# Three-layer feature-cross kernel: fc's columns loaded word by word, dummy products moved and added, and a new order of POOL's first transfers

## The chip, the cores and the metric

The kernel runs on one core of a Trainium2 chip. The metric is the device time of one execution in microseconds; the time before is the median of 8 runs. Five engines work side by side, each on its own list of instructions: TensorE (PE, with its weight loads as PEld), VectorE (DVE), ScalarE (ACT), GpSimd (POOL) and SyncE (SP). SP, ACT and POOL also issue the transfers (DMAs). One execution was also taken by the profiler; all single durations below come from it.

## The reference

The input x has 1024 samples of F = 39 fields with E = 64 values. Three layers each multiply every field of the layer before with every field of x, value by value, and mix the products with a weight table of 64 rows. The sums over E of all three layers' rows go through one linear output, fc.

```python
def _cin_layer(Xk, X0, W, b):
    O = W.shape[0]
    Hk, Fdim = (Xk.shape[1], X0.shape[1])
    Wr = W.reshape(O, Hk, Fdim)
    return jnp.einsum('bhe,bfe,ohf->boe', Xk, X0, Wr) + b[None, :, None]

X0 = sparse_embedding
Xk = X0
outs = []
for W, b in ((W0, b0), (W1, b1), (W2, b2)):
    Xk = _cin_layer(Xk, X0, W, b)
    outs.append(Xk.sum(axis=-1))
cin_output = jnp.concatenate(outs, axis=-1)
return cin_output @ fc_w.T + fc_b
```

fc_w has 192 values: 64 for each layer. Called fc's columns below, they are 64 words each, one for each row of a layer.

## The kernel before

Since the output is linear in the last layer, the kernel folds the weights before it touches the data. fc's third column times W2 gives V2 (one value per row of layer 2 and field; line 338, into the PSUM banks `pv`). V2, with fc's second column beside it as a fortieth column, times W1 gives a second table (line 389, banks `pt` and `pv`). Transposed, it stands in `both` beside the transposed W0 (line 349). From `both`, sums along diagonals (`weight_rows`, lines 436 and 440) and seven 128x128 turns (`weight_turn`, lines 471 and 472) make the stationary operands `wa` of the main part. This is the prologue, some 20 us.

The main part goes through 32 blocks of 32 samples (2048 columns each). A product of two fields is symmetric, so each block needs each pair of fields once; the pairs fill six chunks of 128 rows and half of a seventh, which two blocks share. For each chunk DVE multiplies two gathered copies of the block's rows (`product`, line 164, or 166 for the shared chunk), and TensorE multiplies the result with `wa` (line 487): four 512-column matmuls of two passes each. ACT and DVE finish a block (`finish`, lines 506 to 517): the upper 64 rows plus fc0s, times the lower 64 plus b0s, summed over E. Three small matmuls at the end (line 624) add up the rows of `sums` with `wfin`, which line 532's `last_weights` makes from V2, the biases and `fc`.

The gathered copies are made by POOL with indirect transfers (`gather_rows`, line 125) from tables in device memory that hold a block's 39 rows and a fortieth row of ones. The index lists are worked out by DVE at the start. Block 0 comes in two halves through the tables `xh`, so that the first six gathers (lines 322 to 324) can start before the block is in `xd`; SP copies `xh` into `xd` (line 328). ACT's queue loads W2, xh's first half, W0, W1 and xh's second half, in this order.

The order on each engine is written out by hand: an engine runs its instructions in the order of the program text, and waits where data are missing. On TensorE the prologue is: dummies (`spin`, line 230, products of constants whose result nobody reads), the small products, one dummy, V2 (line 338), W0's transposes (349), W1's product (389), the turns of its result (409), dummies, the first weight turn (471), a dummy, and the main products.

The small products turn fc's row on one partition into columns. SP loads fc_w into `fcrow` (line 193). POOL doubles the third column into `fcrow2` (284) and makes a mask of even and odd rows (281, 282). TensorE turns `fcrow2` (298); DVE writes it, masked, into two columns of `fc2` (301), the stationary operand of V2's product: W2's 64 rows stand there as two halves each, on neighbouring partitions, so column 0 of `fc2` holds fc's column on the even rows and column 32 the same on the odd ones. Five more small products (296) turn the single columns into the PSUM bank `small`, from which ACT copies them into `v2` (362), `fc` (570) and `fc0s` (571).

Of the kernel before, what the change touches and what calls it, by code (L numbers as in the profile page):

```python
# [54 lines left out]
F32 = mybir.dt.float32  # L55
I32 = mybir.dt.int32
# [18 lines left out]
MM = 512  # L75
# [23 lines left out]
def cin_kernel(ctx: ExitStack, tc: tile.TileContext, x, w0t, b0, w1, b1, w2, b2, fc_w, fc_b, out):  # L99
# [39 lines left out]
    fc = const.tile([H, 3], F32, name="fc")  # L139
# [30 lines left out]
    with prep as prep:  # L170
# [4 lines left out]
        fcrow = prep.tile([1, 3 * H], F32, name="fcrow")  # L175
        fcrow2 = prep.tile([1, H, 2], F32, name="fcrow2")
# [6 lines left out]
        parity = prep.tile([128, 2], I32, name="parity")  # L183
        mask = prep.tile([128, 2], F32, name="mask")
# [3 lines left out]
        nc.vector.memset(ones, 1.0)  # L188
        nc.vector.memset(fc2, 0.0)
        nc.vector.memset(v2, 0.0)  # L190
        nc.vector.memset(warm, 0.0)
        w0v = w0t.rearrange("b a h -> b (a h)")
        nc.sync.dma_start(fcrow, fc_w)
# [18 lines left out]
        for i in range(3):  # L212
            for k, by in enumerate((STEP[i + 1], BASE[i + 1], EXTRA[i + 1] - K)):
                nc.gpsimd.memset(shifts[:, k, i : i + 1], float(by))
        for k in range(2):
            nc.gpsimd.dma_start(xh[k][F:FT].rearrange("r (p c) -> p r c", c=128), ones[0:8, 0:1])
# [8 lines left out]
        small = bank("small")  # L225
# [12 lines left out]
        spin(3)  # L238
# [26 lines left out]
        nc.vector.tensor_scalar(parity[:, 1:2], place, 1, None, ALU.bitwise_and)  # L265
# [15 lines left out]
        nc.gpsimd.tensor_copy(mask[:, 1:2], parity[:, 1:2])  # L281
        nc.gpsimd.tensor_scalar(mask[:, 0:1], mask[:, 1:2], -1.0, 1.0, ALU.mult, ALU.add)
        for s in range(2):
            nc.gpsimd.tensor_copy(fcrow2[:, :, s], fcrow[:, 2 * H : 3 * H])

# [3 lines left out]
        for k in range(NTAB):  # L289
            nc.gpsimd.dma_start(xd[k][F::FT].rearrange("r (p c) -> p r c", c=128), ones)  # L290


        one = ones[0:1, 0, 0:1]

        def turn_row(dst, k):
            nc.tensor.matmul(dst, fcrow[:, k * H : k * H + H], one, start=True, stop=True)  # L296

        nc.tensor.matmul(  # L298
            small[:, 0:1], fcrow2.rearrange("p h s -> p (h s)"), one, start=True, stop=True
        )  # L300
        nc.vector.tensor_scalar(fc2[:, 0::32], mask, small[:, 0:1], None, ALU.mult)  # L301
        nc.vector.tensor_scalar(unit, apart, 0, None, ALU.is_equal)
        for k in range(3):
            turn_row(small[0:H, k + 1 : k + 2], k)
        for k in range(2):
            turn_row(small[H:128, k + 4 : k + 5], k)
        spin()
# [14 lines left out]
        for k, cols in enumerate(halves):  # L322
            for i in range(3):
                gather_rows(rt[0][:, i, cols], xh[k], i)
            if not k:
                load(1, nc.gpsimd)
        for k, cols in enumerate(halves):
# [32 lines left out]
        for s, at in enumerate((2, 5)):  # L360
            rows = slice(H * s, H * s + H)
            nc.scalar.copy(v2[rows, s, F:FT], small[rows, at : at + 1])
# [6 lines left out]
        roll(1)  # L369
        for k, t in enumerate((b1, b2)):  # L370
            nc.gpsimd.dma_start(bias[:, k : k + 1], t.rearrange("(h o) -> h o", o=1))
        nc.gpsimd.dma_start(b0s, b0.rearrange("(h o) -> h o", o=1))
        nc.gpsimd.dma_start(fcb, fc_b.rearrange("(p o) -> p o", o=1))
# [14 lines left out]
        for k, a in groups:  # L388
# [6 lines left out]
            )  # L395

# [25 lines left out]
        spin()  # L422
        spin(1, MM // 4)
# [108 lines left out]
    def last_weights(pk):  # L532

        nc.tensor.matmul(pk[0:F, 0:1], v2[0:H, 0, 0:F], bias[:, 0:1], start=True, stop=True)
        nc.tensor.matmul(pk[0:1, 1:2], bias[:, 0:1], fc[:, 1:2], start=True, stop=False)
        nc.tensor.matmul(pk[0:1, 1:2], bias[:, 1:2], fc[:, 2:3], start=False, stop=True)
# [33 lines left out]
    nc.scalar.copy(fc, small[0:H, 1:4])  # L570
    nc.scalar.copy(fc0s[H:128], small[H:128, 4:5])
# [101 lines left out]
```

## Time and profile before

| | |
|---|---|
| median of 8 runs | 749.27 us (748.64 to 749.53) |
| profiled execution: its own time | 749.52 us |
| profiled execution: span | 747.7 us, so 1.8 us lie around it |
| TensorE (PE) busy | 742.8 us, 99% |
| DVE busy | 644.5 us, 86% |
| POOL busy | 321.9 us, 43% |
| ACT busy | 164.6 us, 22% |
| transfers | 180.40 MB, mean 241 GB/s |

How to read the profile's lines: a row of groups gives line, engine, operation, out<-in with partitions x elements and the count, then busy time in us, mean ns of one, then the idle time of that engine just before them and what ended it. The chain of work that ended last is followed back from the last instruction, at each step to what released it. A chain in order of time gives start, length and what ran. A busy PE is not PE at its peak: its clock can be granted at full or at half speed, which the windows view shows as a share in the column after POOL's.

### The profile page before, as it was taken

What the parts mean: (1) busy time and instruction counts of PE and PEld (TensorE: products, weight loads), DVE (VectorE), ACT (ScalarE), POOL (GpSimd) and SP (SyncE); (2) the same over time, 40 slices, a digit from 0 to 9 for tenths busy, and PEclk for the clock granted to TensorE, in tenths of its full rate; (3) what the DMA queues carried; (4) which work ended last, traced back from release to release, by engine and by line L of the source; (5) the groups of instructions that cost most, each with busy time, mean ns of one, the idle gap of its engine ahead of it and who ended that gap; (6) DMA issues with size and microseconds to landing.
All of it is one profiled execution on the core that took longest, in us unless ns stands there. A gap on an engine that the chain in (4) does not pass through costs nothing.

```text
span 747.7 us, 5258 instructions
## 1 busy us (share of the span) xinstructions
PE 742.8 (99%) x1895; PEld 327.4 (44%) x1895; DVE 644.5 (86%) x513; ACT 164.6 (22%) x226; POOL 321.9 (43%) x198
## 2 busy tenths in 40 slices
PE   8999999999999999999999999999999999999998
PEld 6444444444444444444444444444444444444443
DVE  6998889888889888898888889888899888899885
ACT  3132221221212222211221212222112221212222
POOL 7976633336344253633336243263533436243100
PEclk9999999999999999999999999999999999999999
DMA  9999775876657786575876657776565854737400
GB/s 297 345 296 412 258 281 176 330 259 227 277 163 273 250 312 240 182 280 179 338 253 222 270 167 280 259 277 246 190 285 193 337 224 185 283 136 297 168 1 0
DMA packets 58930, 180.40 MB, mean 241 GB/s; under 512 B 37172, under 2 KB 37237, under 8 KB 38808
## 3 DMA queue, kind: packets, MB, share of 16 engines
q0 software_dynamic: 24320, 169.44, 59.8%
q1 hardware_dynamic: 32894, 8.63, 5.0%
q10 hardware_dynamic: 1690, 1.99, 1.0%
q8 instruction: 15, 0.25, 0.1%
q14 instruction: 11, 0.09, 0.0%
HBM read 179.98 MB, written 10.60 MB: 255 GB/s over the span
## 4 chain that ended last, share of the span: by engine, by line
PE 99%; ACT 0%; DVE 0%; issue 0%; ACTq 0%
PE po L487 97%; PE idle L230 1%; PE pt L389 0%; PE pv L338 0%; PE pv L389 0%; PE pw L349 0%; ACT both L418 0%; PE tr L471 0%; ACT part L400 0%; PE small L296 0%; DVE g L526 0%; DVE sums L528 0%; ACT zq L525 0%; PE small L298 0%; DVE fc L301 0%
## 5 line engine op out<-in xcount | busy, mean ns | idle before, releaser
L487 PE MATMUL po<-p,wa 128*128 128x512 f32 (+1 forms) x1792 | 722.7, 595 | 0.0
L164 DVE TENSOR_TENSOR p<-r 128x2048 f32<-128x2048 f32 (+2 forms) x197 | 434.8, 2235 | 85.9 <-PE po L487 85.9
L487 PEld LDWEIGHTS po<-p,wa 128*128 128x128 f32 (+1 forms) x1792 | 313.9, 190 | 405.1 <-issue 384.0
L125 POOL DMA_INDIRECT r<-xd,lists x125 | 253.7, 2030 | 360.6 <-DVE p L164 334.4
L506 ACT ACTIVATE z<-po,fc0s 64x512 f32<-64x512 f32 x124 | 84.6, 683 | 356.5 <-PE po L487 349.7
L500 ACT COPY g<-u 39x1024 f32<-39x1024 f32 x64 | 66.7, 1043 | 180.2 <-DVE sums L517 178.6
L512 DVE SCALAR_TENSOR_TENSOR g<-po,b0s,z 64x512 f32<-64x512 f32 x124 | 86.4, 734 | 0.0
L517 DVE TENSOR_REDUCE sums<-g 103x16 f32<-103x1024 f32 x62 | 75.6, 1220 | 2.2
L166 DVE TENSOR_TENSOR p<-u,v 128x2048 f32<-128x2048 f32 x16 | 36.5, 2284 | 0.0
L125 POOL DMA_INDIRECT u<-xd,lists x16 | 28.9, 1803 | 4.9 <-issue 4.9
L125 POOL DMA_INDIRECT v<-xd,lists x16 | 20.8, 1302 | 4.9 <-issue 4.6
L526 DVE SCALAR_TENSOR_TENSOR g<-po,b0s,zq 64x512 f32<-64x512 f32 x4 | 3.0, 743 | 5.3 <-ACT zq L525 5.3
L230 PE MATMUL idle<-const-float32-1.0 128*128 128x256 f32 (+1 forms) x16 | 6.5, 555 | 0.8 <-PEq L660 0.8
L125 POOL DMA_INDIRECT r<-xh,lists x6 | 5.8, 971 | 1.9 <-issue 1.5
L472 ACT COPY wa<-tr 128x128 f32<-128x128 f32 x7 | 1.9, 266 | 19.4 <-PE tr L471 18.2
L436 DVE TENSOR_TENSOR pairs<-both 128x6 f32<-128x6 f32 (+27 forms) x50 | 5.4, 173 | 0.3 <-ACT both L418 0.3
L119 POOL DMA_DIRECT2D xd<-in_x x5 | 5.2, 1066 | 0.0
L525 ACT ACTIVATE zq<-po,fc0s 64x512 f32<-64x512 f32 x4 | 2.7, 683 | 10.2 <-PE po L487 10.2
L230 PEld LDWEIGHTS idle<-const-float32-1.0 128*128 128x128 f32 x16 | 4.3, 295 | 1.4 <-issue 0.7
L471 PE MATMUL tr<-unit,pairs 128*128 128x128 f32 x7 | 2.2, 319 | 0.9 <-ACT pairs L440 0.9
L528 DVE TENSOR_REDUCE sums<-g 103x8 f32<-103x512 f32 x4 | 2.7, 686 | 0.1
L624 PE MATMUL py<-sums,wfin 103*1 103x512 f32 (+2 forms) x6 | 2.1, 448 | 0.6 <-DVE sums L528 0.6
(95 smaller groups left out, 52.4 us busy)
## 6 DMA issues: line engine op xcount, KB each, us to landing
xd<-in_x SPq DMA_DIRECT2D x26, 312.0 KB
r<-xd,lists POOLq DMA_INDIRECT x125
xd<-in_x POOLq DMA_DIRECT2D x5, 312.0 KB
w2s<-in_w ACTq DMA_DIRECT2D x1, 624.0 KB
w1s<-in_w ACTq DMA_DIRECT2D x2, 312.0 KB
xh<-in_x ACTq DMA_DIRECT2D x2, 156.0 KB
xd<-xh SPq DMA_DIRECT2D x2, 156.0 KB
u<-xd,lists POOLq DMA_INDIRECT x16
```

Source lines behind the costliest of these rows:

```text
L119: engine.dma_start(xd[n // 2 % NTAB][first : first + F].rearrange("f (b e) -> f b e", e=E), xv[:, n * BB : (n + 1) * BB, :],)
L125: nc.gpsimd.indirect_dma_start(dst, None, table, bass.IndirectOffsetOnAxis(ap=lists[:, k : k + 1], axis=0))
L164: nc.vector.tensor_tensor(p[:, cols], r[:, i, cols], r[:, k, cols], ALU.mult)
L166: nc.vector.tensor_tensor(p, ut[n // 2 % 2], vt[n // 2 % 2], ALU.mult)
L230: nc.tensor.matmul(idle[:, 0:cols], nc.const_aps.tensor(1.0, (128, 128), F32), nc.const_aps.tensor(1.0, (128, cols), F32), start=True, sto ...
L436: nc.vector.tensor_tensor(out, diagonal(a, b, sa, sb), diagonal(b, a, sb, sa), ALU.add)
L487: nc.tensor.matmul(po[n + h][m], wa[w, c, :], p[w, bass.ts(m, MM)], start=c == opens[n + h], stop=c == closes[n + h],)
L500: nc.scalar.copy(gt[H : H + F], ut[n // 2 % 2][h : h + F, bass.ts(m, SUB)])
L506: nc.scalar.activation(z[m // 2][:, bass.ts(m % 2, MM)], po[n][m][H:128], AF.Identity, bias=fc0s[H:128])
L512: nc.vector.scalar_tensor_tensor(gt[0:H, at], po[n][m][0:H], b0s, z[m // 2][:, at], ALU.add, ALU.mult)
L517: nc.vector.tensor_reduce(sums[:, b_at : b_at + SB], gt.rearrange("p (b e) -> p b e", e=E), AX.X, ALU.add)
L526: nc.vector.scalar_tensor_tensor(gt[0:H], po[n][m][0:H], b0s, t, ALU.add, ALU.mult)
```

## The change

- fc's third column is loaded as single words straight into `fc2`, 64 words into the even rows by SP, in place of `fcrow`, and the same 64 into the odd rows by POOL, after its first constants. POOL also loads the second column, twice, into `v2`. `fc` (now two columns), `fc0s`, the biases, b0 and fc_b are loaded by SP behind the copies of `xh`; before, the last three went through POOL.
- `fcrow`, `fcrow2`, the mask, the six small products, their dummy, the bank `small` and ACT's copies from it are taken out.
- DVE clears `fc2` and `v2` before it sets `ones`.
- The dummies at the start become four of 256 columns and one of 128 (before, three and one), a dummy of 256 is put behind W1's product, and the dummies behind the turns become two of 256 (before, one of 256 and one of 128).
- POOL's three loads of rows of ones into `xd` move from ahead of the first gather to behind the third gather (the first of them) and behind the gathers of block 1 (the other two).

```diff
@@ -136,7 +136,7 @@
             gather_rows(dst[n // 2 % 2], xd[n // 2 % NTAB], 8 + k)
     wa = const.tile([128, NCHUNK, 2 * H], F32, name="wa")
-    fc = const.tile([H, 3], F32, name="fc")
+    fc = const.tile([H, 2], F32, name="fc")
     v2 = const.tile([128, 2, H], F32, name="v2")
     bias = const.tile([H, 2], F32, name="bias")
@@ -172,25 +172,22 @@
         w1s = prep.tile([128, FH // 2], F32, name="w1s")
         w0s = prep.tile([128, NW * H], F32, name="w0s")
         part = prep.tile([FT, 4 * NA, H], F32, name="part")
-        fcrow = prep.tile([1, 3 * H], F32, name="fcrow")
-        fcrow2 = prep.tile([1, H, 2], F32, name="fcrow2")
         fc2 = prep.tile([128, H], F32, name="fc2")
         ones = prep.tile([16, 2, 128], F32, name="ones")
         warm = prep.tile([1, 1], F32, name="warm")
         place = prep.tile([128, 1], I32, name="place")
         apart = prep.tile([128, 128], I32, name="apart")
         shifts = prep.tile([128, 3, 3], F32, name="shifts")
-        parity = prep.tile([128, 2], I32, name="parity")
-        mask = prep.tile([128, 2], F32, name="mask")
-        nc.vector.memset(ones, 1.0)
         nc.vector.memset(fc2, 0.0)
         nc.vector.memset(v2, 0.0)
+        nc.vector.memset(ones, 1.0)
         nc.vector.memset(warm, 0.0)
         w0v = w0t.rearrange("b a h -> b (a h)")
-        nc.sync.dma_start(fcrow, fc_w)
+        layers = fc_w.rearrange("o (k h) -> h (o k)", h=H)
+        nc.sync.dma_start(fc2[0::2, 0:1], layers[:, 2:3])
         nc.scalar.dma_start(w2s, w2.rearrange("o (s n) -> (o s) n", s=2))
         def load_half(k):
@@ -212,6 +209,9 @@
         for i in range(3):
             for k, by in enumerate((STEP[i + 1], BASE[i + 1], EXTRA[i + 1] - K)):
                 nc.gpsimd.memset(shifts[:, k, i : i + 1], float(by))
+        nc.gpsimd.dma_start(fc2[1::2, 32:33], layers[:, 2:3])
+        for s in range(2):
+            nc.gpsimd.dma_start(v2[H * s : H * s + H, s, F:FT], layers[:, 1:2])
         for k in range(2):
             nc.gpsimd.dma_start(xh[k][F:FT].rearrange("r (p c) -> p r c", c=128), ones[0:8, 0:1])
         nc.gpsimd.iota(apart, pattern=[[1, 128]], base=0, channel_multiplier=-1)
@@ -222,7 +222,6 @@
         pt = [bank("pt") for _ in range(2)] + pv
         idle = bank("idle")
         pw = [bank("pw") for _ in range(2)]
-        small = bank("small")
         def spin(n=1, cols=MM // 2):
@@ -235,7 +234,7 @@
                     stop=True,
                 )
-        spin(3)
+        spin(4)
         spin(1, MM // 4)
@@ -262,7 +261,6 @@
         field = [fields_of[:, i : i + 1] for i in range(6)]
         nc.vector.tensor_scalar(third, place, 171, None, ALU.mult)
         nc.vector.tensor_copy(row, place)
-        nc.vector.tensor_scalar(parity[:, 1:2], place, 1, None, ALU.bitwise_and)
         nc.vector.tensor_scalar(third, third, 9, None, ALU.logical_shift_right)
         step(row, K, 1.0, extra)
         nc.vector.tensor_copy(f0, third)
@@ -278,33 +276,14 @@
         nc.vector.tensor_copy(lists[:, 0:4], fields_of[:, 0:4])
         nc.vector.tensor_scalar(lists[:, 4:8], fields_of[:, 0:4], float(FT), None, ALU.add)
-        nc.gpsimd.tensor_copy(mask[:, 1:2], parity[:, 1:2])
-        nc.gpsimd.tensor_scalar(mask[:, 0:1], mask[:, 1:2], -1.0, 1.0, ALU.mult, ALU.add)
-        for s in range(2):
-            nc.gpsimd.tensor_copy(fcrow2[:, :, s], fcrow[:, 2 * H : 3 * H])
         nc.gpsimd.memset(pairs, 0.0)
         bothv = both.rearrange("p (a b) -> p a b", b=FT)
         nc.gpsimd.memset(bothv[0:H, :, F], 0.0)
-        for k in range(NTAB):
+        def load_ones(k):
             nc.gpsimd.dma_start(xd[k][F::FT].rearrange("r (p c) -> p r c", c=128), ones)
-        one = ones[0:1, 0, 0:1]
-        def turn_row(dst, k):
-            nc.tensor.matmul(dst, fcrow[:, k * H : k * H + H], one, start=True, stop=True)
-        nc.tensor.matmul(
-            small[:, 0:1], fcrow2.rearrange("p h s -> p (h s)"), one, start=True, stop=True
-        )
-        nc.vector.tensor_scalar(fc2[:, 0::32], mask, small[:, 0:1], None, ALU.mult)
         nc.vector.tensor_scalar(unit, apart, 0, None, ALU.is_equal)
-        for k in range(3):
-            turn_row(small[0:H, k + 1 : k + 2], k)
-        for k in range(2):
-            turn_row(small[H:128, k + 4 : k + 5], k)
-        spin()
         step(row, HR, 1.0, half)
@@ -324,6 +303,7 @@
                 gather_rows(rt[0][:, i, cols], xh[k], i)
             if not k:
                 load(1, nc.gpsimd)
+                load_ones(0)
         for k, cols in enumerate(halves):
             nc.sync.dma_start(xd[0][0:F, cols], xh[k][0:F])
         gather_rows(rt[0][:, 3], xd[0][:FT], 3)
@@ -357,9 +337,6 @@
                 pv[k][:, 0:320].rearrange("p (h f) -> p f h", f=10),
             )
         column = blocks.rearrange("h k (f j) -> h (k f) j", j=32)[:, :, 0]
-        for s, at in enumerate((2, 5)):
-            rows = slice(H * s, H * s + H)
-            nc.scalar.copy(v2[rows, s, F:FT], small[rows, at : at + 1])
         for s in range(2):
             rows = slice(H * s, H * s + H)
             nc.vector.tensor_copy(v2[rows, s, 0:20], column[0:H])
@@ -367,10 +344,14 @@
         roll_half(0)
         roll(1)
+        nc.sync.dma_start(fc0s[H:128], layers[:, 0:1])
+        nc.sync.dma_start(b0s, b0.rearrange("(h o) -> h o", o=1))
         for k, t in enumerate((b1, b2)):
-            nc.gpsimd.dma_start(bias[:, k : k + 1], t.rearrange("(h o) -> h o", o=1))
-        nc.gpsimd.dma_start(b0s, b0.rearrange("(h o) -> h o", o=1))
-        nc.gpsimd.dma_start(fcb, fc_b.rearrange("(p o) -> p o", o=1))
+            nc.sync.dma_start(bias[:, k : k + 1], t.rearrange("(h o) -> h o", o=1))
+            nc.sync.dma_start(fc[:, k : k + 1], layers[:, k + 1 : k + 2])
+        nc.sync.dma_start(fcb, fc_b.rearrange("(p o) -> p o", o=1))
+        for k in (1, 2):
+            load_ones(k)
         load(2, nc.gpsimd)
         load(3, nc.gpsimd)
@@ -393,6 +374,7 @@
                 start=True,
                 stop=True,
             )
+        spin()
         for k, a in groups:
             slots = part[:, NA * k : NA * k + NA].rearrange("b (j t) h -> b t j h", t=2)
@@ -419,8 +401,7 @@
                     both[H:128, lo * FT : (lo + n) * FT],
                     turns[k][H * t : H * t + H, (NQ - n) * FT : NQ * FT],
                 )
-        spin()
-        spin(1, MM // 4)
+        spin(2)
         first = [prods.tile([128, BLK], F32, name="p", tag="p") for _ in range(3)]
@@ -532,8 +513,8 @@
     def last_weights(pk):
         nc.tensor.matmul(pk[0:F, 0:1], v2[0:H, 0, 0:F], bias[:, 0:1], start=True, stop=True)
-        nc.tensor.matmul(pk[0:1, 1:2], bias[:, 0:1], fc[:, 1:2], start=True, stop=False)
-        nc.tensor.matmul(pk[0:1, 1:2], bias[:, 1:2], fc[:, 2:3], start=False, stop=True)
+        nc.tensor.matmul(pk[0:1, 1:2], bias[:, 0:1], fc[:, 0:1], start=True, stop=False)
+        nc.tensor.matmul(pk[0:1, 1:2], bias[:, 1:2], fc[:, 1:2], start=False, stop=True)
         nc.vector.memset(wfin[0:H], 1.0)
         nc.scalar.copy(wfin[H : H + F], pk[0:F, 0:1])
         nc.scalar.activation(kfin, pk[0:1, 1:2], AF.Identity, bias=fcb, scale=float(E))
@@ -567,8 +548,6 @@
                     weight_rows(steps[1][1])
         else:
             product(n, c, halves[0], p[n, c])
-    nc.scalar.copy(fc, small[0:H, 1:4])
-    nc.scalar.copy(fc0s[H:128], small[H:128, 4:5])
     for n, c in steps[:3]:
         product(n, c, halves[1], p[n, c])
     n, c = steps[3]
```

## The prediction, made before the change was run

> **What bounds the kernel now.** I read the page's chain first, then the chain of waits over the first 45 us, then busy time by windows (for the granted clock), then the timeline of the first 40 us. The page's fourth part says who sets the end:
>
> ```profile
> PE 99%; ACT 0%; DVE 0%; issue 0%; ACTq 0%
> L487 PE MATMUL po<-p,wa 128*128 128x512 f32 (+1 forms) x1792 | 722.7, 595 | 0.0
> ```
>
> TensorE carries 99% of the chain, and its main products (L487) never wait (0.0). 722.7 of 747.7 us are those products, which the change doesn't touch. So the time moves by as much as the first main product moves, and by the clock at which the first ones run. All is decided before 26 us. The chain of waits there (start, length, what):
>
> ```profile
> 0.77 3.33 PE idle L230 x8
> 4.10 0.53 PE small L298 x2
> ...
> 4.94 0.82 PE small L296 x10
> 5.76 1.15 PE idle L230 x2
> 6.91 2.33 PE pv L338 x8
> 9.24 1.84 PE pw L349 x20
> 11.08 2.43 PE pt L389 x4
> 13.51 1.99 PE pv L389 x4
> ...
> 17.38 0.32 ACT both L418
> ...
> 17.72 0.22 ACT pairs L440
> ...
> 18.65 0.45 PE tr L471
> 19.10 0.85 PE idle L230 x2
> 19.95 1.71 PE po L487 x2
> ...
> 23.83 6.87 PE po L487 x16
> ```
>
> To see: dummies (L230), then the small products that turn fc (L298, L296), a dummy, V2's product (L338), W0's transposes (L349), W1's product (L389), their evictions, the weight table's first turn (L471), the main products. The lengths also give TensorE's rate. Sixteen main passes of 512 columns take 6.87 us, 1192 columns a us. L389's eight passes of 320 take 4.42 us, 579 a us; the first dummies' 1792 columns take 3.33 us, 538 a us. So TensorE runs at half rate until L389's end although it is hardly ever idle. The granted clock in the windows view (the column before the last two) shows the rest:
>
> ```profile
> 18.00:19.00 1.00, 0.35 (x2) 0.38 (x3) 1.00 (x7) 0.00 (x0) 0.69 (x2) 0.80 1.01 414
> 19.00:20.00 1.00, 1.00 (x4) 0.77 (x4) 1.00 (x8) 0.79 (x5) 0.99 (x1) 0.50 1.07 332
> 21.00:22.00 1.00, 1.00 (x3) 0.55 (x2) 1.00 (x6) 0.09 (x1) 1.00 (x1) 0.50 0.97 352
> 22.00:24.00 2.00, 2.00 (x6) 0.83 (x6) 2.00 (x8) 0.30 (x2) 1.69 (x2) 1.00 0.94 242
> ```
>
> The trace's clock record is 1.00 from 15.19, 0.50 from 18.60, 1.00 from 22.02: steps of 3.41 us. So the first 2.1 us of main products ran at half rate. Counted back by that step (an estimate), the earlier edges lie at 11.78, 8.36, 4.95 and 1.54.
>
> **Part by part.**
>
> *Small products.* L298, the wait for DVE's fc2 (4.65), L296 and the dummy behind them occupy TensorE from 4.10 to 6.91. They go; one dummy of 256 columns comes in their place: two passes, 0.85 us at the half rate of the first row. Dummies then end at 4.10 + 0.85 = 4.95, and TensorE could start V2's product 1.96 us earlier. But it needs three things. W2 is there: the trace's completions for w2s end at 4.85. fc2's even rows come by SP: the row nearest, fcrow, was issued at 0.74 and complete at 1.98; with DVE's memset ahead (0.11 us, now first) about 2.3. fc2's odd rows come by POOL, issued when its iota and nine memsets end (1.27). What a 64-word load costs on POOL's sequencer the b1/b2 loads show: 1.18 us for two, 0.59 each. When it lands, nothing shows at this place; the nearest row is xh<-ones (L216), issued at 1.58, complete at 5.90: 4.3 us. So it lands at 5.6. Bounds: 1.24 us as on SP (2.5), 6.4 us as for the load of block 1 on POOL (issued 10.31, complete 16.7), so 7.7. I take 5.6, since that row is of the same queue and moment. V2's product starts at 5.6, 1.3 us earlier, with a TensorE gap of 0.65 us.
>
> The Trainium skill (DMA: Bandwidth & Descriptors, "Anatomy of one DMA") gives a POOL transfer about 2 us fixed, against the row's 4.3; by it the odd rows land near 3.3 and there is no gap. The same page ("Rules for kernel authors") says to coalesce small transfers, which speaks against columns moved word by word; the trace prices a 4-byte packet at 9 ns. By either figure the next paragraph's start stands.
>
> *W1's product.* V2 ends at 5.6 + 2.33 = 7.9. W0's halves are complete at 6.67 and 7.63, so the transposes end at 7.9 + 1.84 = 9.75; V2's turn and copies (10.30 before, 1.06 after V2's product) end at 9.0. But W1's second half completes at 9.83: L389 starts at 9.85, not 11.08: 1.2 us gained, and no faster word could make it more. The 256 new word packets on 16 DMA engines can put W1 off: 16 each at 9 ns is 0.15 us; below nothing, the gathers that now start later free those engines. I take 0.
>
> *The dummy behind L389.* L389 ends at 9.85 + 4.42 = 14.3, the dummy (0.85 at half rate) at 15.15; before, L389 ended at 15.50. So the turns (L409) start 0.35 us earlier, not 1.2. Before, they then waited for ACT's copy of the fourth bank (15.53 to 16.38); now that copy is done at 15.2, and twenty turns 63 ns apart end at 16.45. ACT's copies (L418) start when the second five turns are through, 16.0 against 16.41: 0.4 us earlier. ACT's pairs, DVE's weight rows and the turn L471 follow: 18.25 instead of 18.65. The two dummies behind the turns (0.43 more at full rate) lie in TensorE's 0.86 us wait ahead of L471; uncovered they would cost 0.2 to 0.4.
>
> *Into the half clock.* The main products start about 0.4 to 0.6 us earlier, but up to 22.02 a us is worth half a us: 0.2 to 0.3 us of end time if the edges fall as here, 0.6 if not, 1.2 if the dummy runs at full rate too. I take 0.5.
>
> *POOL.* Ahead of its first gather go the mask (0.24 + 0.19), fcrow2 (0.41) and three ones loads (1.62): 2.46 us. Three word loads come: 1.77 us. POOL is free at 5.55 instead of 6.33. But the gather reads xh's row of ones, whose issue moves behind the word loads, from 1.58 to 3.04; with 4.3 us it lands at 7.4. The first gather goes from 6.72 to about 7.4, later, not freed. One ones load (0.54) now sits before the fourth gather, so the sixth is issued at 15.45 instead of 14.21 and lands at 21.5 instead of 20.3. DVE wants it for the second product's later half near 24.7, now 24.2: 2.7 us of cover. If that were gone, each us late would cost TensorE up to one. The gather of table row 3 still waits for xd<-xh (before: 17.29), behind which its ones row hides (issued about 12, plus 4.3).
>
> *SP, ACT, DVE.* SP's seven word loads stand behind xd<-xh and ahead of nothing until block 4's load; the biases are read by L506 and L512 after 40 us: nothing. Moving four loads (2.4 us) from POOL and bringing two ones loads there (1.1) frees 1.3 us ahead of the loads of blocks 2 and 3; L164's only wait is TensorE (85.9 us), so nothing. ACT loses four copies of 0.15 us off the chain. DVE loses its wait for L298 (1.15 us); its lists come earlier, which the gather can't use.
>
> **Sum.** Against the profiled execution (747.7 span, 1.8 around it, 749.52; 0.25 over the median 749.27): -0.5, so 748.8 by the median.
>
> **Rivals.**
>
> *Faster: L389 or the first main products at full rate.* Until 4.95 TensorE's first step is now 90% or more dummies (before: about 70% dummies, the rest small products), so the clock may rise earlier; or the edges fall so that the longer run of L389 and its dummy (5.3 us, before 4.4) fills a step sooner. Full rate saves 2.1 us on L389's eight passes and 0.4 on the dummy; no half clock after 18.60 saves half of 2.1. The limit is DVE: it ends the fourth product at 29.92, TensorE takes it at 30.65: 0.7 us of slack, and DVE itself comes 0.4 to 1.2 us earlier. So -1.6 to -2.7, about 747.1. Against: what follows the first step (0.65 us gap, V2, transposes) is as thin as what stood between 15.19 and 18.60, and that lost the clock.
>
> The Trainium skill (TensorE: Matmul & The Clock Gate, Part 1) has the full clock after one busy window of 3.4 us, lost after an idle one. By it TensorE, busy here from 0.77 on, should have been fast from about 5 us, and V2 take about 1.2 us; the row has 2.33. So busy time alone doesn't raise it here, and the sum goes by the rows.
>
> *Slower: the words land late.* If 64 words on POOL take the 6.4 us of the long load, fc2 is complete at 7.7, V2's product starts 0.8 us later than before (it decides from 6.9 on), L389 starts at 11.9, and the dummy behind it adds 0.45 that no longer hides: +1.25, and up to +3 if the step from 18.60 isn't filled. About 751.0. For it: that long completion, and full DMA engines (share near 1.0 from 3 us on). Against: L216's rows.
>
> *Slower: a second step at half rate.* Before, TensorE was busy from 18.65 all through the step 18.60 to 22.02. Now L471 and its dummy fall partly ahead of the edge, and about 0.35 us of idleness before the first weights comes inside it (90% busy). If the clock asks for more, the next 3.41 us run at half rate too: +1.7 - 0.2 = +1.5, 750.8.
>
> **How the numbers follow.** The forecast 0.38, the faster rival 0.32, late words 0.17, the second half-rate step 0.13. The forecast's own range, from the uncovered dummies and W1 late (+0.5) to the full 1.2: 748.1 to 749.8. A measurement of this kernel tells about 0.2%, 1.5 us, from no change: under 747.77 is faster, over 750.77 slower. Nearly all of the faster rival is beyond it (0.29), and 0.14 of late words with 0.08 of the second step; the rest is within, 0.49. From 746.6 (the faster rival's end) to 751.1 (late words without the clock's part) about 2 in 10 are left out.
>
> **What would show it.** In the changed profile: V2's product (L338's) near 5.6 behind a gap; L389's first product at 9.8 to 10.1, eight passes in about 4.4 us; the first gather at 7.4, not before 6.7; L471 near 18.25; the clock 0.50 for one step around 18.6 to 22. Wrong if V2 starts after 6.9, if L389 takes under 3 us, if 0.50 is absent or stands for two steps, or if a main product waits for DVE or a gather.

## The result and the profile after

The changed kernel is slower: 751.35 us (median of 12, 749.86 to 752.23) against 749.13 us for the kernel before in the same rounds (32 runs), a ratio of 1.0029 with a 95% interval of 1.0022 to 1.0037. That is 2.2 us more where 0.5 us less was forecast, and 0.25 us above the end of all that the prediction took in (746.6 to 751.1). The profiled execution took 752.15 us, its span is 750.4: 2.7 us over the span before.

The page's chain and the main products' group come first.

```profile
PE 97%; DMA 1%; DVE 0%; ACTq 0%; issue 0%; ACT 0%; DVEq 0%
L468 PE MATMUL po<-p,wa 128*128 128x512 f32 (+1 forms) x1792 | 724.1, 596 | 0.8 <-DVE p L164 0.8
```

A transfer now stands in the chain (DMA 1%), the main products waited 0.8 us where they had waited 0.0, and they were busy 1.4 us longer. The chain of waits up to the first long stretch of main products (start, length, what) answers to the rows of before:

```profile
3.65 7.54 DMA w1s<-in_w
11.19 0.14 issue
11.33 1.68 PE pt L370 x4
13.01 2.13 PE pv L370 x4
15.14 0.75 PE idle L229 x2
...
17.65 0.33 ACT both L400
...
18.06 0.71 DVE pairs L417 x6
18.77 1.25 issue
...
20.09 0.70 DVE p L164
20.80 0.14 issue
20.93 2.05 PE po L468 x2
...
23.19 3.13 PE po L468 x4
...
26.43 6.87 PE po L468 x16
```

Two things are late. W1's product waits for W1, which lands 7.54 us after its issue, and starts at 11.33 (11.01 before, forecast 9.85). Then DVE stands still for 1.25 us ahead of its first product, and TensorE's main products start at 20.93. In the timelines of the two kernels they start 1.18 us apart (19.75 before). The sixteen passes start 2.60 us apart (26.43 against 23.83): the rest was lost in the half clock. The windows view (DVE in the third pair, the granted clock ahead of the last two columns) shows it:

```profile
19.00:20.00 1.00, 1.00 (x3) 0.37 (x3) 0.00 (x0) 0.49 (x3) 0.94 (x1) 0.54 1.06 383
22.00:24.00 2.00, 2.00 (x5) 0.86 (x4) 2.00 (x13) 0.27 (x1) 1.48 (x1) 0.50 0.97 393
24.00:26.00 2.00, 2.00 (x4) 0.74 (x3) 2.00 (x4) 0.00 (x0) 1.70 (x2) 0.52 0.74 233
26.00:28.00 2.00, 2.00 (x7) 0.88 (x6) 1.91 (x3) 0.27 (x1) 1.70 (x2) 1.00 0.99 381
```

0.50 stands for two steps (the trace's record: 19.07 to 25.90), before for one (18.60 to 22.02). Main products ran at half rate from 20.93 to 25.90, 4.97 us, against 2.27 us before (19.75 to 22.02). Half of the 2.70 us more is 1.35, about the 1.4 us of the group's row. With the 1.2 us of later start that is 2.6 of the span's 2.7.

The chain puts DVE's stand to "issue", that is, to nothing that the profile shows. What was late is seen on POOL, in its timeline, here before's two rows and then those of the changed kernel:

```profile
1.58 1.26 POOL L216 DMA_DIRECT2D xh<-ones  x2 [0.31 <-DVE parity L265]
6.72 1.06 POOL L125 DMA_INDIRECT r<-xh,lists  x1 [0.39 <-DVE fields_of L317]
```

```profile
1.64 0.70 POOL L212 DMA_DIRECT2D fc<-in_fc_w  x1 [0.36 <-DVE third L264]
2.34 1.10 POOL L214 DMA_DIRECT2D v<-in_fc_w  x2
3.41 1.09 POOL L216 DMA_DIRECT2D xh<-ones  x2
...
10.90 1.04 POOL L125 DMA_INDIRECT r<-xh,lists  x1 [5.25 <-DMA xh<-ones]
12.25 0.96 POOL L125 DMA_INDIRECT r<-xh,lists  x1 [0.30 <-issue]
```

The three word loads were issued at 1.64, 2.34 and 2.90; by the trace's completions they ended at 6.74, 7.66 and 8.57, 0.9 us apart. The row of ones behind them, issued at 3.41, ended at 10.09. Before, it was issued at 1.58 and ended at 5.90. So the first gather went from 6.72 to 10.90, each time 0.8 us after the end of that row (before's row names DVE for the last 0.39 us).

### The profile page after: what moved, and what is told of

Its sections match the earlier page's. It is cut to its first block, busy times and chain, and to the rows that moved or that the text cites. A ratio compares the mean times of both kernels' runs of the same rounds, so it can differ in the third digit from the quotient of the medians.

```text
span 750.4 us, 5240 instructions
## 1 busy us (share of the span) xinstructions
PE 741.4 (99%) x1885; PEld 325.8 (43%) x1885; DVE 645.0 (86%) x511; ACT 164.0 (22%) x222; POOL 315.3 (42%) x193
## 4 chain that ended last, share of the span: by engine, by line
PE 97%; DMA 1%; DVE 0%; ACTq 0%; issue 0%; ACT 0%; DVEq 0%
PE po L468 96%; DMA w1s<-in_w 1%; PE pv L370 0%; PE pt L370 0%; ACT both L400 0%; ACTq L200 0%; PE tr L452 0%; PE pw L391 0%; DVE g L507 0%; PE idle L229 0%; DVE pairs L417 0%; DVE p L164 0%; DVE sums L509 0%; ACT zq L506 0%; ACTq L194 0%
## 5 line engine op out<-in xcount | busy, mean ns | idle before, releaser
L125 POOL DMA_INDIRECT v<-xd,lists x16 | 15.1, 941 | 4.9 <-issue 4.9
L370 PE MATMUL pt<-w1s,v 128*128 128x320 f32 x4 | 1.7, 554 | 1.9 <-DMA w1s<-in_w 1.9
```

The lines of the kernel that those rows point to most:

```text
L125: nc.gpsimd.indirect_dma_start(dst, None, table, bass.IndirectOffsetOnAxis(ap=lists[:, k : k + 1], axis=0))
```

## The experiments

The theory after the comparison: the loads of single words are the loss, by two ways at once. Way A: on POOL they hold up xh's row of ones, and with it the gathers, until DVE runs out of cover. Way B: while they are under way the large transfers go slower, so W1 comes late. The rival: the words are harmless, and the loss is the dummy behind W1's product, or the clock's edges as they happened to lie. Each experiment was run in five rounds beside the kernel before; times are medians of this kernel / the kernel before. The ratio is taken from the rounds and need not be the quotient of the two medians. The kernel before's own median moved from 748.06 to 749.27 us between sets of rounds, so only ratios compare across sets.

### Are the words the loss, or what came with them?

`e18_change_without_words` is the kernel before, small products and all, with most of the rest of the change: xd's three ones loads behind gathers, the bias loads on SP, the dummies behind W1's product and behind the turns (not the longer start, nor DVE's order).

```diff
+                load_ones(0)            # first of xd's ones loads ahead of a later gather
...
+            load_ones(k)                # the other two, behind block 1's gathers
...
-            nc.gpsimd.dma_start(bias[:, k : k + 1], ...)
+            nc.sync.dma_start(bias[:, k : k + 1], ...)
...
+        spin()                          # behind W1's product
...
-        spin(); spin(1, MM // 4)
+        spin(2)                         # behind the turns
```

> The change without its words: fc's columns by the small products as before, all else of the change that can stand alone (xd's rows of ones behind the gathers, the dummy behind W1's product, two dummies behind the turns, the biases by SP). If the words are the whole loss: within 0.5 us of the kernel before. If the other parts carry some of it: 750 or more, 1 us up.

748.61 / 748.51, ratio 1.0005 (0.9991 to 1.0019). Without the words, and with the small products in their place, the loss is gone. That these two go together leaves a rival: TensorE has nothing to do where the small products stood (idle from 4.97 to 6.83 in the changed kernel), and that may cost clock. Two parts of it alone: `e8_before_dummies` adds only the two dummies to the kernel before, `e4_before_ones_late` only puts xd's ones loads behind gathers.

> The kernel before, with the changed kernel's new dummies alone: one of 256 columns behind W1's product, and two of 256 behind the turns instead of one and a short one. Clock theory (the loss comes from the dummies, which delay the turns by up to 0.85 us): 749.3 to 750, up by 0.5 to 1. Rival (they are hidden behind ACT's copy of the fourth bank): within 0.3 us of the kernel before.

748.21 / 748.06, 1.0005 (0.9990 to 1.0021).

> The kernel before, with only the three loads of xd's rows of ones moved behind the gathers as in the changed kernel. Queue theory: the first gather already waits for xh's row of ones, so it gains at most 0.3 us, nobody waits for it, and the time stays within 0.5 us of 749.1. If these loads mattered (the table's ones row lands late and the gather of row 3 or the products behind it wait), the time rises by 1 us or more. Clock theory: no change.

749.1 / 748.79, 1.0006 (0.9997 to 1.0014). The first gather went from 6.72 to 6.80: as before it starts 0.8 us after xh's ones have landed (5.98), though POOL's sequencer was free long ahead of it. Nothing there could be freed.

The dummy taken out of the changed kernel (`e9_after_no_dummy`, one `spin()` removed behind W1's product):

> The changed kernel without its dummy behind W1's product. If that dummy is part of the loss (it keeps TensorE 0.4 to 0.85 us ahead of the turns), the turns start up to 0.85 us earlier; but DVE's first product still waits for the late gather, so by the queue theory the time stays within 0.4 us of the changed kernel, 2 us over the kernel before. Rival (the dummy is the loss): 1 us or more off.

750.98 / 748.24, 1.0043 (1.0028 to 1.0057). The loss stays; the rival of the dummy falls.

### Way A: the gathers

`e6_before_xh_ones_late` has no word at all: the kernel before, with xh's two ones loads moved behind xd's three. `e16_before_xh_ones_mid` moves them half as far, behind the copies of fcrow2.

```diff
-        for k in range(2):
-            nc.gpsimd.dma_start(xh[k][F:FT]..., ones[0:8, 0:1])
...
         (e16: behind fcrow2's copies; e6: behind xd's ones)
+        for k in range(2):
+            nc.gpsimd.dma_start(xh[k][F:FT]..., ones[0:8, 0:1])
```

> The kernel before, with POOL's two loads of xh's rows of ones moved behind the three of xd, right ahead of the first gather; no words, the small products as they were. It makes the first gathers late and nothing else: the first at about 11 us. Queue theory: DVE's first product waits for the second gather as in the changed kernel, the first main product starts 0.5 to 1.5 us later, and the time rises by 0.8 to 2 us to 749.7 to 751. Rival (late gathers cost nothing, the words and W1 do): 748.8 to 749.2.

750.62 / 748.06, **1.0033** (1.0020 to 1.0047): 2.6 us, the whole size of the change's loss. In its view of waits the wait has a name (who <- what it waited for: us in total, times, longest):

```profile
DVE p L164 <- DMA r<-xh,lists: 3.0, 1, 3.0
...
PE po L487 <- DVE p L164: 2.4, 1, 2.4
```

The first gather came at 11.79, DVE's first product at 19.19 after 3.05 us of waiting, and the clock record shows two half-rate steps (16.29 to 23.12), as in the changed kernel.

> The kernel before, with xh's rows of ones behind fcrow2's copies: the first gather at about 9 to 9.5 us, half as late as with the loads right ahead of the gathers (11.8, which cost 2.5 us). By the prediction's cover (the second gather lands at 13.7 and the product reads it at 18.5) this costs nothing: within 0.4 us of the kernel before. If every us of lateness counts: 1 to 1.3 us up.

749.11 / 748.84, 1.0005 (0.9993 to 1.0018), with the first gather at 9.21. So 2.5 us of lateness costs nothing that can be told and 5.1 us costs 2.6; the changed kernel's 4.2 us lies between, behind the end of the cover.

### Way B: W1, with the gathers on time or early

`e1_ones_first` puts xh's ones ahead of the three word loads on POOL; `e5_ones_between` puts them behind fc2's word and ahead of v2's two.

```diff
+        for k in range(2):                       # e1: moved up to here
+            nc.gpsimd.dma_start(xh[k][F:FT]..., ones[0:8, 0:1])
         nc.gpsimd.dma_start(fc2[1::2, 32:33], layers[:, 2:3])
                                                  # e5: ones here
         for s in range(2):
             nc.gpsimd.dma_start(v2[...], layers[:, 1:2])
-        for k in range(2):
-            nc.gpsimd.dma_start(xh[k][F:FT]..., ones[0:8, 0:1])
```

> The changed kernel, with the two loads of xh's rows of ones issued on POOL ahead of the three word loads instead of behind them. Queue theory (the rows of ones stand behind the words in POOL's transfer queue, so the first gather starts 4.2 us late, DVE's first product waits for it, and the clock loses a second step): the first gather starts near 7 us, no wait of DVE for a gather at the first product, the first main product at 19 to 19.8 us instead of 20.9, the time 748.5 to 749.6. W1 theory (the words hold up W1's load, which lands at 11.2 instead of 9.8, and that is what moves the start): W1's product still starts at 11.3 and the time stays at 751 to 751.5. Clock theory (the new dummies alone shift the half-rate steps): the time stays at 751 to 751.5 with two half-rate steps behind 18 us.

750.6 / 748.79, 1.0025 (1.0012 to 1.0037). The first gather is at 7.00, so the queue's order is right, but now fc2's word is late. Its chain of waits:

```profile
2.92 5.85 DMA fc<-in_fc_w
...
8.87 2.40 PE pv L318 x8
```

V2 starts at 8.87: with this order it is V2 that waits, and the gain on the gathers is gone. (This profile is of the slowest of ten executions, 755.87 us, so only its order of events is read here.)

> The changed kernel, with POOL's first transfers in the order fc2's odd words, xh's two rows of ones, v2's words (two word loads fewer ahead of the rows of ones). Queue theory (a 64-word load holds POOL's transfer queue for about 0.9 us, so two fewer bring the rows of ones forward by about 2 us): V2 still starts at 6.8, the first gather goes from 10.9 to about 9 us, DVE's first product no longer waits for it, the first main product starts at 19.4 to 20 and the time is 749.3 to 750.3, at least 1 us under the changed kernel. Rival (W1's late load and the clock make the loss, the gathers don't): 751 to 751.5 as before this edit.

749.75 / 748.06, 1.0024 (1.0011 to 1.0036). V2 at 6.43, first gather at 8.87 (inside the cover), no wait of DVE: way A is closed, and 1.7 us of loss stay. W1's product starts at 11.34, and the record's first full step only at 16.00. The same without the dummy, `e10_between_no_dummy`:

> The order fc2, ones, v2 on POOL and no dummy behind W1's product: both suspected costs taken away, W1 still late at 11.1. Queue theory with W1 as what is late next: the turns start at 15.5 as in the kernel before, the first main product at 19.3 to 20, the time within 0.7 us of the kernel before. Rival (the words cost something else as well): 1.2 us or more above the kernel before, as with the dummy.

750.5 / 748.24, 1.0030 (1.0016 to 1.0044): W1's product at 12.45. Here it isn't W1 that comes last (it landed at 11.92) but v2's second word load, which this order puts behind the ones: issued at 3.95, landed at 12.10, and the chain runs through it. So closing way A gains nothing that can be told from the changed kernel's 1.0029, while late gathers without a word (e6) cost as much: the ways lie side by side and don't add up. What the rest with way A closed is made of, W1, v2's words or the clock, these two don't tell.

The transfers in the windows view (DMA share and GB/s last), from 5 to 6 us: the kernel before, the changed kernel, and e18 without words.

```profile
5.00:6.00 1.00, 1.00 (x11) 0.98 (x12) 0.86 (x9) 0.52 (x1) 1.00 (x3) 1.00 1.10 318
```

```profile
5.00:6.00 1.00, 0.00 (x0) 0.00 (x0) 0.91 (x4) 0.58 (x1) 0.65 (x2) 1.00 0.52 188
```

```profile
5.00:6.00 1.00, 1.00 (x11) 0.98 (x12) 0.86 (x9) 0.84 (x1) 0.00 (x0) 1.00 1.01 275
```

The engines moved 188 GB/s at half their share where they move 318 and 275. e9 shows the same hole earlier and deeper, with 55 GB/s from 4 to 5 us. Summed from 4 to 7 us, the engines moved 0.41 to 0.75 MB in the nine profiles with words issued in the first 2.8 us, and 0.74 to 0.87 in the eleven others. When do words do this? The next four add unread 64-word loads to the kernel before, at other moments and on other queues. `e3_before_words`: three on POOL ahead of xh's ones.

```diff
+        words = prep.tile([128, 3], F32, name="words")
...
+        for s in range(3):
+            nc.gpsimd.dma_start(words[0:H, s : s + 1], layers[:, 2:3])
         for k in range(2):
             nc.gpsimd.dma_start(xh[k][F:FT]..., ones[0:8, 0:1])
```

> The kernel before, with three 64-word loads that nobody reads put on POOL's queue ahead of xh's rows of ones (they go into a spare tile; all else as before). Queue theory: the first gather moves from 6.7 to about 11, the first product waits for it, and the time rises by 1.5 to 2.5 us to 750.7 to 751.6. W1 theory: W1 lands later by up to 1.4 us, its product starts at about 11.3 instead of 11.0, and the time rises by 0.3 at most. Clock theory: no change, 749.1.

751.01 / 748.79, 1.0027 (1.0016 to 1.0038), but by more than was meant: POOL's copies of fcrow2 also went back (to 5.15), and V2 started at 8.39. First gather 11.81, W1's last packet at 11.0. `e14_before_early_words` has them just behind xh's ones (issued 2.84 to 3.92), with mask and fcrow2's copies given to DVE; `e11_before_words_behind` behind the copies (4.72 to 5.87).

> The kernel before, with three unread 64-word loads on POOL right behind xh's rows of ones (issued at 2.9 to 4.6 us), and the mask and fcrow2's copies made by DVE, so that the small products don't stand behind POOL's issuing. Left is what early words do to W1 and to POOL's later transfers. W1 theory: W1's last packet ends at 10.1 to 11, its product starts at 11.3 to 12, the time rises by 0.5 to 1.5 us with the first gather still at about 7. Gather theory alone (only late rows of ones cost): within 0.4 us of the kernel before.

750.83 / 748.84, 1.0027 (1.0010 to 1.0044), and again not by the words: DVE took 2.02 us for the two copies that POOL had done in 0.41, and V2 started at 8.56 in its profile (of the slowest of twelve executions, 755.24 us, at half rate up to 29.04). What it does say is that W1 was on time, its last packet at 9.51.

> The kernel before, with three unread 64-word loads on POOL behind fcrow2's copies and xh's rows of ones, ahead of xd's rows of ones: neither the small products nor the first gather stand behind them (the first gather at about 8.5 us, which has cover). Left is what the words do to other transfers. W1 theory: W1 completes at 11 or later instead of 9.8 to 10.4 and its product starts up to 0.5 us later, the time 0.2 to 0.8 us up. Queue theory alone: within 0.3 us of the kernel before.

747.46 / 748.24, 1.0004 (0.9989 to 1.0019): words this late cost nothing that can be told. W1's last packet 9.45.

`e13_before_sp_words` adds one 64-word load on SP behind fcrow's row; `e2_words_sp` gives SP all four words of the changed kernel.

> The kernel before, with one unread 64-word load on SP's queue right behind fcrow (as the changed kernel has one there), nothing on POOL. If early words as such slow the other transfers, the transfer engines move under 220 KB in one of the microseconds from 4 to 7 (260 to 300 before), W1's last packet ends at 10 or later instead of 9.4 to 9.7, and the time rises by 0.2 to 1 us. If only POOL's queue is slow with words: no change in W1, the time within 0.4 us of the kernel before.

749.79 / 748.84, 1.0011 (1.0003 to 1.0020). W1's last packet came at 10.33 and its product at 11.46. Yet this profile is of the fastest of its eleven executions (748.28), with the full clock from 9.54: there the late W1 alone cost nothing that shows.

> The changed kernel, with all four word loads on SP's queue and none on POOL's. Queue theory: POOL's first transfer is xh's row of ones again, the first gather starts at 6.8 to 7.2 us and the time falls to 748 to 749.5. W1 theory: the same 256 words still cross the transfer engines, W1 lands near 11.2 and the time stays at 751. Clock theory: stays at 751.

753.98 / 748.79, 1.0058 (1.0035 to 1.0081), the worst of all, and no clean test: with more of SP's transfers under way ACT issued W1's two loads later, at 5.07 and 6.54 (3.09 and 3.65 in the changed kernel), each after the SP transfer that had its semaphore ended (4.87 and 6.52). In e13 too W1's second load went out late, at 4.89 instead of 3.64, after W2's load, which had its semaphore there (4.87).

Over all twenty profiles W1's last packet ends at 9.30 to 10.06 in the eleven without words issued in the first 2.8 us (before among them), and at 10.09 to 11.0 in the nine with such words (the changed kernel among them). The two groups don't overlap, though their nearest members are 0.03 us apart, and in e2 and e13 the late issue has its part. So early words and a late W1 go together. But W1 is late without them too: of the kernels without early words, seven have W1's product wait for W1, and it starts at 10.32 (e11) to 11.14 (e4), against 11.33 in the changed kernel.

```profile
10.32 1.96 PE L393 MATMUL pt<-w1s,v 128*128 128x320 f32 x4 [1.88 <-DMA w1s<-in_w]
11.14 2.47 PE L392 MATMUL pt<-w1s,v 128*128 128x320 f32 x4 [2.17 <-DMA w1s<-in_w]
11.33 1.68 PE L370 MATMUL pt<-w1s,v 128*128 128x320 f32 x4 [1.86 <-DMA w1s<-in_w]
```

What W1's lateness alone costs isn't shown: `e17_before_w1_late`, which was to price it by loading xh's second half ahead of W1, missed.

```diff
+        load_half(1)
         (the two loads of W1)
-        load_half(1)
```

> The kernel before, with ACT's load of xh's second half moved ahead of W1's two loads; no words, the rows of ones and the small products as they were. It makes W1 late and little else (xh's second half earlier, which nobody waits for). If W1's lateness is a cost of its own: W1's product starts at 11.5 to 12.5 instead of 10.3 to 11.1 and the time rises by 0.6 to 2 us, 1.0008 to 1.0027 of the kernel before. If only late gathers cost: within 0.4 us.

748.47 / 748.51, 1.0002 (0.9985 to 1.0019). W1's last packet came at 9.59: it wasn't late, so this says nothing.

### The clock

`e7_filled` is e5 with the waits filled by dummies: seven at the start in place of four and a short one, three more ahead of W1's product.

> The kernel of the order fc2, ones, v2 with more dummies: seven at the start instead of four and a short one, and three ahead of W1's product, so that TensorE is busy over both waits (for fc2's words and for W1). Clock theory: with both gaps filled the clock stays at full rate from the first step on, W1's product takes 2.2 us instead of 4, no half-rate step falls into the main products' start, and the time is 746.5 to 748.5. Rival (the clock is lost anyway in the transposes and the gap ahead of the first turn, and the dummies only delay the products): 750 to 751.5.

749.05 / 748.06, 1.0009 (0.9996 to 1.0023). The granted clock is 1.00 from 3.87 on. The ratio falls from e5's 1.0024 to 1.0009, 0.7 us by the medians, with intervals that overlap. W1's product stays late, at 11.64, again behind v2's second word load (landed at 11.29). So with way A closed and TensorE's waits filled no loss is left that can be told, though the words are all there.

The same on the kernel before. `e12_before_filled` moves the five single-column products (`turn_row`) behind V2's product, ahead of W0's transposes, with `spin(2)` in their place and `spin(2)` behind the transposes, ahead of W1's product; `e15_filled_more` has four there, and three behind the turns.

```diff
-        (five turn_row(small[...]) and spin() ahead of V2)
+        spin(2)
...
+        (the five turn_row(small[...]) behind V2's product)
...
+        spin(4)                 # ahead of W1's product; e12: spin(2)
...
-        spin(); spin(1, MM // 4)
+        spin(3)                 # behind the turns; e15 only
```

> A try at a better kernel: the kernel before, with the five small products that turn the single columns moved behind V2's product, two dummies instead of them and one dummy ahead of V2, and two dummies ahead of W1's product. Clock theory (TensorE must be filled with full-size products for a whole step of 3.41 us, then it runs at full rate; the small products are what keeps the first steps from it): V2 and W1's product run at full rate in most executions and the time falls by 1 to 3 us, to 745.5 to 747.5. Rival (the transposes and the gap before the first turn lose the clock again, or V2 starts later by the extra dummies): 0 to 1 us slower than before.

747.03 / 748.24, 0.9993 (0.9974 to 1.0011): nothing that can be told.

> The try at a better kernel again, with two more dummies ahead of W1's product (four) and three of 256 columns behind the turns instead of one and a short one. Clock theory: the steps in which TensorE waits for W1 and for the first weights are filled too, more executions stay at full rate, and the time falls to 745.8 to 747.2, 1 to 2 us under the kernel before. Rival (at half rate the extra dummies run past W1's landing and delay its product by up to 1.5 us): the same as before or up to 1 us slower.

747.74 / 748.84, **0.9984** (0.9975 to 0.9992): 1.1 us faster than the kernel before, and the only kernel here whose interval lies below 1. Its chain of waits and a stretch of its windows view:

```profile
3.63 7.31 DMA w1s<-in_w
...
11.08 1.40 PE pt L390 x4
12.48 1.16 PE pv L390 x4
```

```profile
22.00:24.00 2.00, 1.96 (x6) 0.69 (x6) 2.00 (x3) 0.27 (x1) 2.00 (x1) 1.00 1.01 385
```

W1's product starts no earlier than before (11.08) but takes 2.56 us where it took 4.42, and no main product runs at half rate (1.00 from 4.33 on in the record, to the main products' end). The interval is not clear of e12's, so how much the further dummies add isn't shown.

## Why the prediction was wrong

**Small products and V2: right in direction, mis-sized.** The two parts of fc2's words were to be there at 5.6. V2 started at 6.83, only 0.01 us earlier than in before's timeline. The row chosen (xh<-ones, 4.3 us) was of the same queue, but the word took 5.1 us there (1.64 to 6.74), and POOL issued it 0.37 us later than the 1.27 assumed.

**W1 there at 9.83 and untouched by words: the step that failed, with its cost not settled.** The prediction priced 256 packets at 9 ns on 16 engines, 0.15 us, and took 0. W1's product started at 11.33 where 9.85 was forecast. Of the 1.2 us to be gained at least 0.5 were never there: 9.83 is the last of only seven completion marks that before's trace keeps of that load, where the changed kernel's keeps sixteen, the last at 11.19; without early words the product that waits for W1 starts at 10.32 to 11.14. That leaves 0.2 to 1.0 us for the words (an estimate from these starts). The price of a packet in an engine says nothing of what a load of 64 of them does to the transfers beside it: the rate fell from 318 to 188 GB/s. The rule that the prediction cited from the Trainium skill (DMA: Bandwidth & Descriptors, "Rules for kernel authors"), to coalesce small transfers, was set aside on that 9 ns; e18, with fc_w as one row again, against the changed kernel speaks for the rule, as far as it can (see what stays open).

**POOL: the second step that failed.** xh's ones were to land 4.3 us after their issue whatever lay ahead, so at 7.4, and the 2.7 us of cover was counted for the sixth gather only. They landed 6.7 us after issue, at 10.09, behind three loads that ended 0.9 us apart. The sign named for this, "the first gather at 7.4, not before 6.7", gave 10.90, and a main product waited for DVE, which was named as what would make it wrong. That the gathers would not be freed was right (e4), and that there is some cover too: 2.5 us cost nothing that can be told (e16). (POOL's own terms add up to 5.64, not 5.55; nothing hangs on it.)

**Dummies: right.** They cost nothing that can be measured (e8, e9), though the one behind W1's product stands in the changed kernel's chain with 0.75 us, as the prediction had it.

**Clock: the edges were no property of the kernel, the third step that failed.** The estimate counted 3.41 us steps back from one profile and took them as fixed. The step is right, its place isn't. e4 gives TensorE the same work as before up to V2, and its record is 1.00 from 4.19, where before's is from 15.19; V2 takes 1.38 us there and 2.40 in before. From before's row the prediction argued against the page TensorE: Matmul & The Clock Gate, Part 1 (full rate after one busy window of 3.4 us, with a window that runs freely); e4, and the changed kernel with 1.00 from 5.42, go with the page. e5 has the changed kernel's filled start and 1.00 only from 16.0. Counted back from each record (an estimate), dummies up to 4.97 fill 2.96 of the 3.41 us from 2.01 to 5.42 in the changed kernel, and 2.61 of those from 2.36 to 5.77 in e5: where the edges fall decides. Counted so in all twenty profiles, up to W1's product: each step at half rate that held 2.86 us or more of dummies and V2's product was followed by full rate, none with 2.67 or less; in before the fullest holds 2.67 (4.95 to 8.36). The faster rival's first half did come true: V2 ran at full rate in the changed kernel's profile. But the clock was lost again at 12.25, behind a step (8.84 to 12.25) that held the wait from 9.47 to 11.33: 1.86 us of idleness, not the whole idle window of the page.

**The rivals.** Late words was the right mechanism in the wrong place. V2 stayed below the 6.9 us from which that rival was to decide; the lateness went into the loads behind and beside the words. The second half-rate step came too, and its 750.8 is nearer to the result than the forecast; what lay inside the first step was not 0.35 us of idleness, but 0.84 us of waiting for DVE.

**What stays open.** How the 2.2 us divide between gathers, W1 and clock. The profile gives 1.2 of later start and 1.4 of half rate, but for one execution, and the mean granted clock of the others can't divide theirs: it counts the time ahead of the record's first full step as full (0.999 in e14's profile, at half rate up to 29.04). Nor does any clean run part the words from the idle time that the small products left: e18 takes away both, e3 and e13 add words alone but make V2 or W1's second load late by another way, and e7, which fills the waits, points to the idle time without showing it. DVE's 1.25 us in the changed kernel is put down to "issue" there; that it is the gather rests on e6 (named) and e16 (gone). And why words issued before 2.8 us should slow W1, while those from 2.84 on left it on time, wasn't found.

## What to carry to other kernels

A transfer is priced by what waits behind it in its queue and runs beside it, not by its packets alone: before putting a small strided load in front of others, list whose landing each later wait needs, and how much cover it has. A row of another transfer gives a landing time only for the same number of loads ahead of it. A completion read from a trace is only as good as the marks that the trace keeps of it: compare several profiles. A few us of a start-up phase that depend on the granted clock can't be read from one profile; here filling TensorE's waits (e15) gained 1.1 us where the change, meant to shorten them, lost 2.2.

## What the runs showed of the hardware

- A 64-word column load on POOL took 5.1 us from issue to completion, and the next ones ended 0.9 us apart. On SP the column of fc2's even rows took 4.0 us (0.97 to 4.99), where the same kind of queue brought fcrow as one row in 1.24 us.
- One more transfer on SP moved ACT's issue of W1's second load from 3.64 to 4.89 (e13), four words on SP moved it to 6.54 (e2): in this kernel the two queues draw on the same semaphores, and a load waits for the transfer that had its own (ended at 4.87 and 6.52).
- Two copies of 64 elements took DVE 2.02 us (3.68 to 5.70) while POOL issued transfers and then filled tiles (2.84 to 5.62, e14), and POOL 0.41 us in before.
- Full clock was first recorded anywhere from 3.65 to 17.01 us across these profiles, and once at 29.04 (e14), in kernels that began with much the same dummies. Ahead of it the windows view shows 1.00 too, though before's V2 took 2.40 us there and e4's, behind its first full step, 1.38.
- Up to W1's product, half rate ended only behind a 3.41 us step that held 2.86 us or more of dummies and V2's product; 2.67 us were not enough (twenty profiles, the steps counted back from each record, an estimate).
